# Attention scores by seven block products, partial sums copied out of the PSUM banks, and a fixed order of all engines in attention

## The chip, the cores and the metric

The kernel runs on one core of a Trainium2 chip. The core has a matrix engine (TensorE, PE in the profile, with its weight loads as PEld), VectorE (DVE), ScalarE (ACT), GpSimd (POOL) and SyncE (SP, which issues transfers). Matrix products are written to PSUM, 8 banks of 512 fp32 values a partition; all other data of a stage lies in SBUF. The metric is the time of one execution on the device in microseconds.

## What is computed

A macaron block on x of shape (2, 2048, 256) in fp32: half a feed-forward, attention, half a feed-forward, each on the layer norm of x, each added to x.

```python
x = x + 0.5 * ffn(layernorm(x), w_gate, w_up, w_down)
x = x + attn(layernorm(x), Wq, bq, Wk, bk, Wv, bv, Wo, bo)
x = x + 0.5 * ffn(layernorm(x), w_gate, w_up, w_down)

def ffn(x, w_gate, w_up, w_down):          # every operand rounded to fp4 in blocks of 16, 704 hidden
    h = silu(fp4_linear(x, w_gate)) * fp4_linear(x, w_up)
    return fp4_linear(h, w_down)

def attn(x, ...):                          # one head; complex q, k, v of 256 each, so 512 real columns
    scores = (qr @ kr.T + qi @ ki.T) / sqrt(256)
    w = softmax(scores)
    return stack([w @ vr, w @ vi]) @ Wo.T + bo
```

## The kernel before

The 4096 tokens are 32 tiles of 128, 16 for each batch element ("batch" below). The kernel runs the first feed-forward (FFN0), the attention and the second feed-forward (FFN1), which overlap at their seams. Query and key weights are folded into one 256 x 256 matrix `wa`, value and output weights into `wvo`, so attention works on the normalised x itself: `xT` (x transposed, the keys) and `xn` (x as it is, the values).

**Attention's steps.** Queries go in 8 groups of 512 (`Group`, four to a batch), keys in `NP = 8` pairs of tiles. A *step* `n = 8 gi + s` is group `gi` against key pair `s`. In step n PE computes

- `scores` (L889): for each of the pair's two key tiles a 128 x 512 block of scores, two matmuls of 512 columns each, into a PSUM bank of `p_acc`; ACT copies the block to SBUF (L896, the *piece* `st`), and DVE takes the running maximum `most` from PSUM (L901);
- `values` (L969) of step n - 10, seven matmuls of 256 columns: the 2 x 2 block product of weights and values is made by seven block products instead of eight (the groups but the last), whose left sides are the `xn` blocks with their sums s1 to s4 (`plain`), and whose right sides are quarters of the piece and sums `tw` of them, made by DVE in `combined` (L933, L936, L937).

In between, the group's maximum is transposed (`peak`, L908), reduced, spread over the partitions (`highest`, L915) and copied by ACT from PSUM to SBUF (`top`, L917). `weights` subtracts it from a piece (DVE, L921) and takes the exponential (ACT, L922), one piece a step, one group behind the scores. When the eight values steps of a group are through, `collect` (L988 to L995) puts the seven products together and `close` (L1002 to L1008) multiplies by `wvo`, divides by the sum of weights and adds to x, four tiles at once.

**PSUM.** `p_big` has two tiles of two banks (the seven products `m`, or a feed-forward's gate and up), `p_t` two banks for all transposes, queries and closings, `p_acc` two banks (scores, last group's values, down projections).

**Other work beside the steps.** Batch 1 is normalised, transposed (`turned`, L826) and laid out (`plain`) during the groups of batch 0, and the first inputs of FFN1 are rounded during the last groups.

**What sets the order.** In FFN0 and FFN1 strings (`FFN0_ORDER`, `FFN1_ORDER`) say which piece of work issues its next instruction, and `fence` holds each engine to that order. In attention there is no such string: a scheduler orders the instructions by their dependencies and by marks, with which `tc.issue_after` (L1019, L1091) ties a step's side work to the step's last maximum or last matmul:

```python
seen, scored = scores(todo[gi], s) if gi < groups else (None, None)
with behind(seen):
    if 0 < gi < groups:
        shifted(todo[gi - 1], s)
```

## Time and profile before

| | |
|---|---|
| three runs | 1030.5, 1031.86, 1032.02 us, median 1031.86 |
| the profiled execution | 1032.48 us, span 1029.9 us, mean granted clock 0.998 |
| PE busy | 1002.9 us, 97% of the span |
| DVE, ACT, POOL busy | 785.6, 418.3, 165.6 us |
| 320 to 770 us (attention alone) | PE 449.2, DVE 317.0, ACT 200.7, POOL 5.8 of 450 us |
| matmuls of the scores (L889) | 512 records, 231.8 us |
| matmuls of the values, seven products (L969) | 784 records, 224.5 us |
| DMA in 320 to 770 us | 1 GB/s |

An fp32 matmul leaves two records on PE, and two weight loads. "Busy" is the share of time in which an engine executes; for PE the ends of records are modelled. In the groups, a line names the source line, the engine, the operation, the tiles (out<-in) and the shapes, then busy time and the mean duration of one in ns, then the engine's idle time just before it and what ended that. The chain of waits follows the work that ended last back to the start; the timeline gives start and length of each instruction, with the idle time before it and its releaser in brackets.

### The profile page before, as it was taken

To read this page: it belongs to the slowest core of one execution; us is meant where nothing else is said; L and a number is where in the kernel's file an instruction comes from. 1 tells how busy PE (TensorE), PEld (TensorE's weight loads), DVE (VectorE), ACT (ScalarE), POOL (GpSimd) and SP (SyncE) were. 2 spreads that over 40 slices of the span, in tenths; PEclk is the share of its full clock that TensorE was granted. 3 is DMA by queue.
4 is the path that set the end of the run, shared out by engine and by line. 5 is a ranking of instruction groups with operands and counts; after the bars stand their busy time and mean duration, and the time that the engine had idled before them with its cause. 6 is when DMAs were issued, how large, how long until landed. Compare 5 with 4: busy or idle time off the path is not lost.

```text
span 1029.9 us, 10476 instructions
## 1 busy us (share of the span) xinstructions
PE 1002.9 (97%) x3813; PEld 690.7 (67%) x3813; DVE 785.6 (76%) x1329; ACT 418.3 (41%) x651; POOL 165.6 (16%) x94
## 2 busy tenths in 40 slices
PE   5999999999999999999999999999999999999997
PEld 3667667767665667667676766666655666776776
DVE  7999999969744977476677867677757389988895
ACT  5755533343326543246444533343333244333121
POOL 4464133131220000000000000000002102133321
PEclk9999999999999999999999999999999999999999
DMA  9001246433420000000000000000000033664552
GB/s 321 9 1 48 65 100 108 94 84 63 100 59 1 1 0 1 1 1 0 1 1 1 0 1 1 1 0 1 1 0 1 11 74 92 123 138 109 125 122 57
DMA packets 59285, 49.30 MB, mean 48 GB/s; under 512 B 46050, under 2 KB 51171, under 8 KB 58851
## 3 DMA queue, kind: packets, MB, share of 16 engines
q1 hardware_dynamic: 58272, 48.11, 20.1%
q10 hardware_dynamic: 962, 0.53, 0.2%
q8 instruction: 30, 0.49, 0.2%
q14 instruction: 21, 0.16, 0.0%
HBM read 8.46 MB, written 4.19 MB: 12 GB/s over the span
## 4 chain that ended last, share of the span: by engine, by line
PE 83%; DVE 12%; ACT 2%; issue 1%; DMA 1%; ACTq 0%; DVEq 0%
PE gu L525 22%; PE ps L889 21%; PE m L969 16%; PE po L581 13%; PE poa L1002 3%; PE z L947 3%; PE pu L871 3%; DVE h L242 2%; DVE qh_s L223 1%; PE th L566 1%; DVE bn L321 1%; PE txa L826 1%; DVE h L234 1%; DVE h L543 1%; DMA x<-in_x_dram 1%
## 5 line engine op out<-in xcount | busy, mean ns | idle before, releaser
L525 PE MATMUL gu<-wgu,xqT 128*128 128x352 f32 x992 | 305.7, 460 | 2.7 <-issue 0.7
L525 PEld LDWEIGHTS gu<-wgu,xqT 128*128 128x128 f32 x992 | 185.5, 190 | 101.3 <-issue 5.7
L889 PE MATMUL ps<-uT,xT 128*128 128x512 f32 x512 | 231.8, 593 | 0.2
L581 PE MATMUL po<-wd,hqT 128*128 128x256 f32 x768 | 175.4, 382 | 0.0
L581 PEld LDWEIGHTS po<-wd,hqT 128*128 128x128 f32 x768 | 145.3, 192 | 26.0 <-issue 2.4
L889 PEld LDWEIGHTS ps<-uT,xT 128*128 128x128 f32 x512 | 95.4, 190 | 94.3 <-issue 80.0
L901 DVE TENSOR_TENSOR most<-ps,most 128x512 f32<-128x512 f32 x112 | 77.3, 690 | 104.4 <-ACT st L896 104.0
L896 ACT COPY st<-ps 128x512 f32<-128x512 f32 x128 | 74.6, 583 | 153.3 <-PE ps L889 153.2
L969 PE MATMUL m<-tw,xn 128*128 128x256 f32 x448 | 124.5, 379 | 0.0
L251 POOL TENSOR_TENSOR hqT<-hqT,qh_t 128x1408 f32<-128x1408 f32 x24 | 76.0, 3166 | 191.9 <-DMA qh_t<-h 145.2
L969 PE MATMUL m<-st,xn 128*128 128x256 f32 x336 | 100.0, 379 | 0.0
L969 PEld LDWEIGHTS m<-tw,xn 128*128 128x128 f32 x448 | 85.1, 190 | 12.5 <-DVE tw L933 0.6
L922 ACT ACTIVATE st<-st 128x1024 f32<-128x1024 f32 x64 | 67.2, 1056 | 64.4 <-DVE st L921 64.1
L539 ACT ACTIVATE h<-gu 128x704 f32<-128x704 f32 x62 | 46.6, 756 | 102.5 <-PE gu L525 99.1
L543 DVE TENSOR_TENSOR h<-h,gu 128x704 f32<-128x704 f32 x62 | 54.3, 878 | 40.9 <-PE gu L525 31.2
L969 PEld LDWEIGHTS m<-st,xn 128*128 128x128 f32 x336 | 63.3, 190 | 26.1 <-issue 19.1
L921 DVE TENSOR_TENSOR st<-st,top 128x1024 f32<-128x1024 f32 x64 | 77.0, 1216 | 2.4 <-ACT top L917 2.4
L303 POOL TENSOR_TENSOR xl<-xl,qx_s 128x1024 f32<-128x1024 f32 x4 | 7.8, 1944 | 381.7 <-DVE xl L301 381.7
L239 ACT ACTIVATE qh_m<-h 128x1408 f32<-128x1408 f32 x24 | 33.0, 1376 | 57.5 <-DVE h L234 37.3
L234 DVE SCALAR_TENSOR_TENSOR h<-h,qh_r 128x1408 f32<-128x1408 f32 x24 | 49.0, 2043 | 0.3
L583 DVE SCALAR_TENSOR_TENSOR x<-po,x 128x256 f32<-128x256 f32 x64 | 26.1, 413 | 30.2 <-PE po L581 30.2
L242 DVE SCALAR_TENSOR_TENSOR h<-qh_m,h 128x1408 f32<-128x1408 f32 x24 | 42.6, 1776 | 1.8 <-ACT qh_m L239 1.8
(181 smaller groups left out, 1115.1 us busy)
## 6 DMA issues: line engine op xcount, KB each, us to landing
hqT<-eight SPq DMA_DIRECT2D x24, 704.0 KB
xqT<-eight SPq DMA_DIRECT2D x9, 512.0 KB
out_dram<-x SPq DMA_DIRECT2D x15, 256.0 KB
x<-in_x_dram SPq DMA_DIRECT2D x3, 1024.0 KB
eight<-whole SPq DMA_DIRECT2D x24, 44.0 KB
wd<-wd SPq DMA_DIRECT2D x2, 384.0 KB
n_down<-in_w_down_dram SPq DMA_DIRECT2D x1, 704.0 KB
n_up<-in_w_up_dram SPq DMA_DIRECT2D x1, 640.0 KB
```

The source lines that it names most:

```text
L234: nc.vector.scalar_tensor_tensor(yb, yb, BELOW, rec.unsqueeze(2).to_broadcast([P, nb, BLK]), ALU.mult, ALU.mult)
L242: nc.vector.scalar_tensor_tensor(y, m, LEAST, y, ALU.max, ALU.add)
L251: nc.gpsimd.tensor_tensor(state["dst"], state["dst"], crossed, ALU.mult)
L525: nc.tensor.matmul(out=ps[:, b2, 0:HALF], lhsT=xqT[:, i % XT, kc, :], rhs=wgu[:, kc, ts(which * 2 + b2, HALF)], start=(kc == 0), stop=(kc ...
L543: nc.vector.tensor_tensor(h, h, up, ALU.mult)
L581: nc.tensor.matmul(out=po, lhsT=hqT[:, r, :], rhs=right, start=(k == 0), stop=(k == NR - 1))
L889: scored = nc.tensor.matmul(out=ps, lhsT=gr.of.xT[s][:, c, v, :], rhs=gr.uT[:, c, :], start=(c == 0), stop=(c == KD - 1),)
L896: nc.scalar.copy(piece[:, v, :], ps)
L901: seen = nc.vector.tensor_tensor(gr.most, ps, gr.most, ALU.max)
L921: nc.vector.tensor_tensor(piece, piece, gr.top.unsqueeze(1).to_broadcast([P, 2, Q]), ALU.subtract)
L922: nc.scalar.activation(piece, piece, AF.Exp, scale=SCALE)
L969: i = nc.tensor.matmul(out=gr.m[k], lhsT=left, rhs=right, start=first, stop=last)
```

## The change

**Scores.** For steps n = 10 to 63 (`PLAIN = 10` and on) a new function `step(n)` takes the place of `scores`, `shifted`, `combined`, `values`, `queries`, `close` and `peak` in the loop. The pair's two key tiles and the two halves of the 256 features form a 2 x 2 block matrix, the group's queries (two halves of 256 queries) another; their product is made by seven block products of 256 columns instead of four matmuls of 512. The partial sums share registers: `px` and `pz` are the halves of the step's bank `ps`, `py` is the second half of the bank of the step before. `px` is read three times while it accumulates: after products 1 (ACT, L1212), 2 (ACT, L1230) and 3 (DVE, L1248); `pz` twice (ACT L1213, DVE L1237). The fourth product into `px` is issued in the next step (`deferred`, L1164) and copied there (L1215).

**Sums of keys and queries.** The left sides need four sums of key blocks a pair (`halves`, tiles `xS`), the right sides four sums a group (`halved`, in `uT`), all on POOL. The four sums of the value step move from DVE to POOL (`combined`), one of them in place in the piece.

**Maxima.** `most` is now taken from the piece's two halves in SBUF (L1251 for the upper, `seen_lower` in the next step for the lower). `top` stays in PSUM: the ACT copy goes, and DVE's subtraction (`lowered`, L1048) reads it there. While a top is held, transposes, queries and closings have one bank of `p_t` instead of two (`bank`).

**Order.** The whole region n = 10 to 63 is fenced: every engine executes its instructions in the order in which `step` writes them. Side work (batch 1's statistics, `turned`, `halves` and `plain`, FFN1's first inputs) is cut into turns, and `spare` issues turns at three places of a step, up to a budget for each engine (0.7 and 1.25 us of DVE; 2.0 us for each of ACT, DVE, POOL and PE at the end). Closings are made one tile at a time in steps s = 3 and 4, queries at s = 2 (or 4 and 5).

**Smaller parts.** The ring of pieces has 11 places instead of 12; `xn` has 7 blocks instead of 8, one of them restored by POOL for the last group; the reciprocal root of the variance is a power on POOL for batch 1 and FFN1's first groups instead of ACT's square root and DVE's reciprocal.

The diff, cut to its core (lines that only pass `bank` for the pool, and `queries`, `close`, `plain` cut into turns, are left out):

```diff
+    def bank(shape, name):
+        passing["turn"] ^= 1
+        tag = "t1" if passing["top"] or passing["turn"] else "t0"
+        return p_t.tile(shape, FP, tag=tag, name=name)
...
+            if self.power:
+                nc.gpsimd.tensor_tensor(rstd, var, minus_half[:, 0:n], ALU.pow)
+                yield "W"
+            else:
+                nc.scalar.activation(sd, var, AF.Sqrt)
+                yield
+                nc.vector.reciprocal(rstd, sd)
+                yield
...
+            y = xl.rearrange("p u d -> p (u d)")
+            nb = XT * D // BLK
+            yb = y.rearrange("p (b k) -> p b k", k=BLK)
+            yield "W", 0
+            yield "D", 1.2
+            scale = xp.tile([P, nb], FP, tag="qx_s", name="qx_s", bufs=2)
+            nc.vector.tensor_reduce(scale, yb, AX.X, ALU.max, apply_absolute_value=True)
+            yield "D", 0.7
+            rec = xp.tile([P, nb], FP, tag="qx_r", name="qx_r", bufs=2)
+            nc.vector.tensor_scalar(scale, scale, 1.0 / 6.0, TINY, ALU.mult, ALU.max)
+            nc.vector.reciprocal(rec, scale)
+            yield "D", 1.2
+            by_block = rec.unsqueeze(2).to_broadcast([P, nb, BLK])
+            nc.vector.scalar_tensor_tensor(yb, yb, BELOW, by_block, ALU.mult, ALU.mult)
+            yield "A", 1.0
+            m = xp.tile([P, XT * D], FP, tag="qx_m", name="qx_m", bufs=1)
+            nc.scalar.activation(m, y, AF.Abs, scale=STEPS)
+            yield "W", 0
+            yield "D", 1.2
+            nc.vector.scalar_tensor_tensor(y, m, LEAST, y, ALU.max, ALU.add)
+            yield "D", 1.2
+            nc.vector.scalar_tensor_tensor(y, m, LEAST, y, ALU.max, ALU.subtract, reverse1=True)
+            yield "W", 0
+            yield "G", 1.9
+            nc.gpsimd.tensor_tensor(yb, yb, scale.unsqueeze(2).to_broadcast([P, nb, BLK]), ALU.mult)
+            yield "W", 0
...
+        def halves(self, p, pool):
+            yield "W", 0
+            x, t = self.xT[p], pool.tile([P, 4, P], FP, tag=f"xS{p}", name=f"xS{self.b}_{p}")
+            self.xS[p] = t
+            a11, a12, a21, a22 = x[:, 0, 0, :], x[:, 1, 0, :], x[:, 0, 1, :], x[:, 1, 1, :]
+            add = nc.gpsimd.tensor_tensor
+            yield "G", 0.9
+            add(t[:, 0, :], a21, a22, ALU.add)
+            add(t[:, 1, :], t[:, 0, :], a11, ALU.subtract)
+            yield "G", 0.9
+            add(t[:, 2, :], a11, a21, ALU.subtract)
+            add(t[:, 3, :], a12, t[:, 1, :], ALU.subtract)
+        def restored(self, p):
+            yield "G", 0.6
+            a11, s3 = self.xn[p][:, 0, :], self.xn[p][:, 1, :]
+            nc.gpsimd.tensor_tensor(s3, a11, s3, ALU.subtract)
+            nc.gpsimd.memset(s3[:, P - 1:P], 1.0)
...
-    RING = NP // 2 + LAG
+    RING = NP + LAG + 1
+    EARLY = 6
+    PLAIN = NP + LAG
...
+        def halved(gr):
+            b11, b12, b21, b22, t1, t2, t4 = (gr.uT[:, k, :] for k in range(7))
+            add = nc.gpsimd.tensor_tensor
+            add(t1, b12, b11, ALU.subtract)
+            yield
+            add(t2, b22, t1, ALU.subtract)
+            yield
+            add(t4, b21, t2, ALU.subtract)
+            yield
+            add(b12, b22, b12, ALU.subtract)
+            yield
...
+            passing["top"] = True
+            gr.top = p_t.tile([P, QG, P], FP, tag="t0", name=f"top{gr.i}")
             for u in range(QG):
-                nc.tensor.transpose(pt[:, u, :], gr.mx[:, u:u + 1].to_broadcast([P, P]), ident)
-            gr.top = late["pool"].tile([P, Q], FP, tag="top", name=f"top{gr.i}")
-            nc.scalar.copy(gr.top, pt.rearrange("p u s -> p (u s)"))
+                nc.tensor.transpose(gr.top[:, u, :], gr.mx[:, u:u + 1].to_broadcast([P, P]), ident)
+        def lowered(gr, s):
+            piece = gr.pieces[s]
+            top = gr.top.rearrange("p u s -> p (u s)").unsqueeze(1).to_broadcast([P, 2, Q])
+            nc.vector.tensor_tensor(piece, piece, top, ALU.subtract)
+        def raised(gr, s):
+            piece = gr.pieces[s]
+            nc.scalar.activation(piece, piece, AF.Exp, scale=SCALE)
         def weights(gr, s):
-            piece = gr.pieces[s]
-            nc.vector.tensor_tensor(piece, piece, gr.top.unsqueeze(1).to_broadcast([P, 2, Q]), ALU.subtract)
-            nc.scalar.activation(piece, piece, AF.Exp, scale=SCALE)
+            lowered(gr, s)
+            raised(gr, s)
...
-        def combined(gr, s):
-            piece = gr.pieces[s]
-            b = piece.rearrange("p v (h q) -> p (v h) q", h=2)
-            t = late["pool"].tile([P, 4, HQ], FP, tag="tw", name=f"tw{gr.i}_{s}", bufs=2)
-            nc.vector.tensor_tensor(
-                t[:, 0:2, :], b[:, 0:4:3, :], b[:, 1:2, :].to_broadcast([P, 2, HQ]), ALU.add
-            )
-            nc.vector.tensor_tensor(t[:, 3, :], t[:, 1, :], b[:, 0, :], ALU.add)
-            nc.vector.tensor_tensor(t[:, 2, :], t[:, 3, :], b[:, 2, :], ALU.add)
-            gr.t[s] = t
...
+        def combined(gr, s, engine):
+            b = gr.pieces[s].rearrange("p v (h q) -> p (v h) q", h=2)
+            gr.t[s] = t = late["pool"].tile([P, 3, HQ], FP, tag="tw", name=f"tw{gr.i}_{s}", bufs=2)
+            add = engine.tensor_tensor
+            add(t[:, 0, :], b[:, 0, :], b[:, 1, :], ALU.add)
+            add(b[:, 1, :], b[:, 3, :], b[:, 1, :], ALU.add)
+            add(t[:, 1, :], b[:, 1, :], b[:, 0, :], ALU.add)
+            add(t[:, 2, :], t[:, 1, :], b[:, 2, :], ALU.add)
...
+        def deferred():
+            gr, s, ps, piece, _ = pend.pop("fourth")
+            nc.tensor.matmul(
+                out=ps[:, 0:HQ], lhsT=gr.of.xT[s][:, 1, 1, :], rhs=gr.uT[:, 6, :], start=False, stop=True,
+                skip_group_check=True,
+            )
+        def seen_lower(gr, s, piece):
+            if s == 0:
+                nc.vector.tensor_tensor(most_of(gr), piece[:, 1, :], piece[:, 0, :], ALU.max)
+            else:
+                nc.vector.tensor_tensor(gr.most, piece[:, 1, :], gr.most, ALU.max)
+        def step(n):
+            gi, s = divmod(n, NP)
+            gr, old = todo[gi], todo[gi - 1]
+            gv, sv = divmod(n - NP - LAG, NP)
+            valued = sevenfold(todo[gv], sv)
+            x, sums, u = gr.of.xT[s], gr.of.xS[s], gr.uT
+            a11, a12, a21, a22 = x[:, 0, 0, :], x[:, 1, 0, :], x[:, 0, 1, :], x[:, 1, 1, :]
+            piece = room(gr, s)
+            b = piece.rearrange("p v (h q) -> p (v h) q", h=2)
+            if "bank" not in pend:
+                pend["bank"] = p_acc.tile([P, Q], FP, tag="acc", name="ps")
+            ps = p_acc.tile([P, Q], FP, tag="acc", name=f"ps{gi}_{s}")
+            before = pend["bank"]
+            px, pz, py = ps[:, 0:HQ], ps[:, HQ:Q], before[:, HQ:Q]
+            asks = gi + 1 < groups and (gi + 1) % (tiles // QG) != 0
+            if s == 2 and gi + 1 < groups:
+                todo[gi + 1] = Group(gi + 1)
+            ahead = todo.get(gi + 1)
+            def times(out, left, right, start=False, stop=False):
+                nc.tensor.matmul(out=out, lhsT=left, rhs=right, start=start, stop=stop, skip_group_check=True)
+            def v(k):
+                for _ in range(k):
+                    next(valued, None)
+            late_one = s in (0, 2)
+            if s == 3 and asks or s == 6 and ahead and not asks:
+                all_of(halved(ahead))
+            times(px, a11, u[:, 0, :], True)
+            times(pz, sums[:, 0, :], u[:, 4, :])
+            fourth = pend.get("fourth")
+            if fourth:
+                deferred()
+            nc.scalar.copy(b[:, 0, :], px)
+            nc.scalar.copy(b[:, 3, :], pz)
+            if fourth:
+                nc.scalar.copy(fourth[4], before[:, 0:HQ])
+            if "exp" in pend:
+                raised(*pend.pop("exp"))
+            cs, cn = divmod(n - NP - LAG + 1, NP)
+            combined(todo[cs], cn, nc.gpsimd)
+            early = not late_one and n > NP + LAG
+            if early:
+                lowered(old, s)
+            spare(n, "D", 0.7)
+            if s == 2 and asks:
+                queries(ahead, 0)
+            elif s != 2:
+                v(1)
+            times(px, sums[:, 1, :], u[:, 5, :])
+            times(pz, sums[:, 3, :], u[:, 3, :])
+            nc.scalar.copy(b[:, 1, :], px)
+            if fourth:
+                seen_lower(fourth[0], fourth[1], fourth[3])
+            v(1)
+            if s == 0:
+                pt = peak(old)
+            v(1)
+            nc.vector.tensor_tensor(b[:, 1, :], pz, b[:, 1, :], ALU.add)
+            if s == 0:
+                peaked(old, pt)
+            times(px, sums[:, 2, :], u[:, 1, :])
+            times(py, a12, u[:, 2, :], True, True)
+            if early:
+                raised(old, s)
+            if s == 0:
+                highest(old)
+            else:
+                spare(n, "D", 1.25)
+            nc.vector.tensor_tensor(b[:, 3, :], px, b[:, 3, :], ALU.add)
+            nc.vector.tensor_tensor(b[:, 0, :], py, b[:, 0, :], ALU.add)
+            if s > 0:
+                nc.vector.tensor_tensor(gr.most, piece[:, 0, :], gr.most, ALU.max)
+            if s == 2 and asks:
+                queries(ahead, 1)
+            if late_one and n > NP + LAG:
+                lowered(old, s)
+                pend["exp"] = old, s
+            if s in (3, 4) and "closing" in pend:
+                close(pend["closing"], 2 * (s - 3))
+            v(7)
+            if s in (4, 5) and ahead and not asks:
+                queries(ahead, s - 4)
+            if s in (3, 4) and "closing" in pend:
+                close(pend["closing"], 2 * (s - 3) + 1)
+                if s == 4:
+                    pend.pop("closing")
+            if sv == NP - 1:
+                pend["closing"] = todo.pop(gv)
+                collect(pend["closing"])
+            pend["bank"] = ps
+            pend["fourth"] = gr, s, ps, piece, b[:, 2, :]
+            spare(n, "ADGP", 2.0)
...
+            if PLAIN <= n < groups * NP:
+                if n == PLAIN:
+                    begun = len(nc.cur_bb.bb.instructions)
+                step(n)
+                if n == groups * NP - 1:
+                    fourth = pend["fourth"]
+                    deferred()
+                    nc.scalar.copy(fourth[4], fourth[2][:, 0:HQ])
+                    seen_lower(fourth[0], fourth[1], fourth[3])
+                    peaked(fourth[0], peak(fourth[0]))
+                    fence(begun)
+                yield None, None
+                continue
...
+    def spare(n, kinds, most):
+        left = {kind: most for kind in kinds}
+        for task in list(asides):
+            if task[0] > n:
+                continue
+            if task[2][0] == "W":
+                task[2] = next(task[1], None)
+            while task[2] is not None and task[2][0] in left and task[2][1] <= left[task[2][0]]:
+                left[task[2][0]] -= task[2][1]
+                task[2] = next(task[1], None)
+            if task[2] is None:
+                asides.remove(task)
+            elif task[2][0] != "W":
+                left.pop(task[2][0], None)
...
+    def turned(b, p):
+        turns = batches[b].turned(p, kt)
+        for kind in "AAWPP":
+            yield kind, 0.5
+            if kind != "W":
+                next(turns)
+        yield from batches[b].halves(p, late["pool"])
...
+    LED = 4
+    for p in range(LED, NP):
+        aside(EARLY + p, batches[0].plain(p, late["pool"]))
+    for p in (6, 7, 0, 1):
+        aside(PLAIN, batches[0].halves(p, late["pool"]))
+    for part in range(tiles // GT):
+        aside(PLAIN, counted(batches[1].measure(part)))
+    for p in range(NP):
+        aside(per - NP + 1 + p, turned(1, p))
+    for p in range(NP):
+        aside(per + LAG + 1 + p, batches[1].plain(p, late["pool"]))
+    aside(per + NP + LAG + 2, first_inputs())
+    for p in range(NP):
+        aside((groups - 1) * NP + LAG + 1 + p, batches[NB - 1].restored(p))
```

## The prediction

> **What bounds the kernel now.** I read the table of engines first, then the chain that ended last, the stretches, the groups, and one step of attention instruction by instruction. TensorE (PE) is busy 97% of the span, so what counts is the time in which it works or waits:
>
> ```profile
> PE 1002.9 (97%) x3813; PEld 690.7 (67%) x3813; DVE 785.6 (76%) x1329; ACT 418.3 (41%) x651; POOL 165.6 (16%) x94
> PE gu L525 22%; PE ps L889 21%; PE m L969 16%; PE po L581 13%; PE poa L1002 3%; PE z L947 3%; PE pu L871 3%; DVE h L242 2%; DVE qh_s L223 1%; PE th L566 1%; DVE bn L321 1%; PE txa L826 1%; DVE h L234 1%; DVE h L543 1%; DMA x<-in_x_dram 1%
> ```
>
> The stretches show that inside attention PE has no gap at all and GpSimd (POOL) next to no work (columns: stretch, length, busy time of PE, weight loads, DVE, ACT, POOL, granted clock):
>
> ```profile
> 350.00:400.00 50.00, 50.00 (x181) 33.33 (x180) 38.60 (x93) 19.33 (x27) 0.00 (x0) 1.00 0.00 1
> 650.00:700.00 50.00, 50.00 (x190) 34.35 (x189) 34.22 (x57) 20.33 (x31) 0.63 (x1) 1.00 0.00 1
> ```
>
> The chain there is a plain alternation of a step's scores (8 records) and values (14 records), start and length in us:
>
> ```profile
> 603.10 3.43 PE ps L889 x8
> 606.53 3.02 PE m L969 x14
> 609.55 3.43 PE ps L889 x8
> ```
>
> So a step costs PE 3.43 + 3.02 = 6.45 us, and nothing else costs anything. One fp32 matmul is two records: 3.43/4 = 0.858 us for 512 columns, 3.02/7 = 0.432 for 256. The durations of what the change touches (mean ns behind the bar):
>
> ```profile
> L896 ACT COPY st<-ps 128x512 f32<-128x512 f32 x128 | 74.6, 583 | 153.3 <-PE ps L889 153.2
> L921 DVE TENSOR_TENSOR st<-st,top 128x1024 f32<-128x1024 f32 x64 | 77.0, 1216 | 2.4 <-ACT top L917 2.4
> L922 ACT ACTIVATE st<-st 128x1024 f32<-128x1024 f32 x64 | 67.2, 1056 | 64.4 <-DVE st L921 64.1
> L988 ACT COPY u<-m x7: 354/372/373, 385.9 to 738.8; 128x256 f32<-128x256 f32 x7
> L991 DVE TENSOR_TENSOR u<-m,u x7: 415/417/423, 388.5 to 740.7; 128x256 f32<-128x256 f32 x7
> ```
>
> And the handovers, from the step at 662, with start and length:
>
> ```profile
> 662.38 3.60 PE L889 MATMUL ps<-uT,xT 128*128 128x512 f32 x8
> 664.35 0.58 ACT L896 COPY st<-ps 128x512 f32<-128x512 f32 x1 [1.26 <-PE ps L889]
> 664.97 0.69 DVE L901 TENSOR_TENSOR most<-ps,most 128x512 f32<-128x512 f32 x1 [1.45 <-ACT st L896]
> 702.35 0.89 PE L1002 MATMUL poa<-wvo,zT 128*128 128x257 f32 x3 [0.60 <-DVE x L1008]
> ```
>
> The first two matmuls end at 662.38 + 1.72 = 664.10; ACT starts 0.25 later (0.20 in the median, where no event is waited for as well); DVE starts 0.04 after ACT's end (664.93). The L1008 before 702.35 ended at 702.20 (start 701.72, 0.48 long): DVE to PE 0.15 with two waits; elsewhere 0.055 with one.
>
> **The change, part by part.**
>
> *Seven products.* For n = 10 to 63, 54 steps, four matmuls of 512 become seven of 256: 7 x 0.432 = 3.02 instead of 3.43. Gain 0.41 x 54 = 22.3 us if PE stays without a gap.
>
> *The partial sums.* They are read while the accumulation goes on, and every such read stands on PE's path, since the next product into that bank waits for it. The order on PE becomes: px, pz (1, 2); the fourth product of the step before, in another bank (3); a value (4); px, pz (5, 6); two values (7, 8); px (9); py in the other bank (10); four values. The waits attached to the changed instructions: (5) waits for ACT, that is for both copies L1212 and L1213; (9) waits for DVE's add L1237, which reads pz next to px and itself waits for the copy L1230. Two gaps follow:
> - 2 to 5: PE has (3) and (4), 0.863 us. Needed: 0.20 + 0.055 (L1212 waits for two more semaphores) to the first copy's start, 0.272 to the start of the next (0.372 less 0.10 of overlap, as ACT's back-to-back copies start), 0.372, and 0.055 back to PE: 0.95, with another event on the second wait 0.99. Stall 0.13. At s=2 the first query matmuls stand here, 1.73 us, and hide it. 47 steps: 6.1 us.
> - 6 to 9: again 0.863. Needed: 0.20 + 0.372 + 0.03 + 0.418 + 0.055 = 1.08. Stall 0.21, and 0.27 with one more event; I take 0.24. At s=0 four transposes hide it. 48 steps: 11.5 us.
> - 10 to the next 1: L1248 and L1249, 0.20 + 0.33 + 0.42 + 0.06 = 1.0, under 1.73 us of values. Nothing.
>
> Bounds: both hidden, 0; or both 0.15 longer for further events and queued work, 17.6 + 0.15 x 95 = 32 us.
>
> *ACT's queue.* A step has four copies of 256 and an exp: 4 x 0.37 + 1.06 = 2.5 of 6 us. But what is put between the exp and L1212 delays L1212 and, through (5), PE. For n = 26 to 32 the asides of batch 1 put the copy of xT (0.58) and two norms (0.50 apart) there: the transposes end with the step, so the copy starts 0.20 into the next one and L1212 comes at 0.20 + 0.58 + 1.04 = 1.82 instead of 1.16. 7 x 0.66 = 4.6 us. At n = 48 and 54 the Abs of FFN1's input (1.06) waits for DVE's product before it (1.21) and stands ahead of L1212: some 1.65 each, 3.3. None of the three existed as a stall before, where the scheduler placed them; bounds 0 and twice.
>
> *DVE's queue.* Out go a step's sums for the values (three instructions, 0.68 + 0.42 + 0.47 by the groups tw); in come three adds of 0.42; the two maxima of 0.69 stay, now from SBUF alone. So DVE holds 1.22 + 1.26 + 1.38 = 3.9 of 6.4 us, and is no bound. The statistics of batch 1 at n = 44 to 45 and the row of one closing tile stand ahead of L1237 once: 1.3, between 0 and 2.6.
>
> *POOL.* The four sums of 256 move here, with the halves of keys and queries. Trace rows of POOL give 1.06 us for 512 and 2.59 for 1408, undisturbed, so 0.19 us + 1.7 ns an element: 0.63 for 256, as an estimate (the ends: 0.5, half of 1.06, and 1.06 itself). 4 x 0.63 + gaps = 2.8 of 6.4 us, with the halves of keys (4 x 0.41) or queries (4 x 0.63) 4.6 to 5.5, with FFN1's product (1.95) 4.8: it fits, and the results are wanted a step later; at 1.06 it would not in those steps, which the rival below prices. The power that takes the place of a root and a reciprocal for batch 1 has no row; it works on 8 elements a partition, so between 0.2 (POOL's copies of 4) and 1.2 (its smallest sum), and is wanted some steps later: 0. The table loads of 1.28 that the root cost ACT go with it, gain 0 to 2.6, taken as 0, for ACT's idle time before its copies was 153 us. No DMA is issued in these steps and SP's queue is passed by nothing. What speaks against POOL is the company:
>
> ```profile
> 699.37 1.95 POOL L303 TENSOR_TENSOR xl<-xl,qx_s 128x1024 f32<-128x1024 f32 x1 [49.87 <-DVE xl L301]
> 699.84 1.76 DVE L937 TENSOR_TENSOR tw<-tw,st 128x256 f32<-128x256 f32 x1
> ```
>
> L937, 0.42 otherwise, took 1.76 and ended 0.28 after POOL, while the L901 at 546.86, one input of which is in PSUM, kept its 0.69 inside POOL's L303 of 545.39 to 547.33. Of the new DVE work only the two maxima have both inputs in SBUF. The first stands ahead of L1237 with 0.3 to 0.5 us to spare, one add of POOL is 0.63: a quarter of the steps may lose 0.2, 2.7 us at most; I take 0 and keep 2.7 in the range. Weighed against the Trainium skill, "SBUF — State Buffer", section "Who interferes with whom": there a VectorE instruction with two SBUF inputs contends with a GpSimd instruction that reads SBUF, and the loser is blocked for a whole instruction. This is what the row shows. By that rule read strictly, each maximum that meets an add would lose up to 0.63, and the sum would be 0.3 x 54 = 16 us worse; by the row and the slack it is the 0 to 2.7 above.
>
> *Small ones.* Start of the new order at n = 10, whose sums DVE still made: +1. The end of n = 63, where the last product, its copy, a maximum and the transposes follow one another: 0.43 + 0.2 + 0.37 + 0.69 + 0.1 = 1.8, less what PE does meanwhile: +1.45. PE's own few stalls of before (two of 0.17, one of 0.77) go: -1.1. The single bank for transposes while the maximum stays in PSUM, the pieces' ring of 11, and FFN1's inputs: each has a step of time to spare; 0, bounds -2 and +3.
>
> Sum: -22.3 + 6.1 + 11.5 + 4.6 + 3.3 + 1.3 + 1.0 + 1.45 - 1.1 = +5.9. The profiled execution took 1032.48 (span 1029.9, 2.6 around it), 0.6 above the median of 1031.86; so about 1038.4 by its clock, 1037.8 in the median. I say 1038.
>
> **The rivals.**
> - *The copies are hidden* (faster). If the handovers between 2 and 5 and between 6 and 9 are 0.13 and 0.24 shorter than added up, both gaps vanish: -22.3 + 10.6 = -11.7; without the waits in ACT's queue too, -19.6. Time 1012 to 1020. For it: the gaps are small beside the 1.0 us that I added up, and the weight loads go ahead of a waiting matmul, as the timeline of before shows. Against: each part of the sums is a measured row. It decides at 11.7/54 = 0.22 us of both gaps together in a step: below that the change gains.
> - *POOL and DVE hold each other up.* If the first maximum mostly meets an add, or POOL takes 1.06 rather than 0.63 and the values wait for its sums, 0.3 to 0.5 us a step: +16 to +27 more, 1054 to 1065. For it: L937's 1.76. Against: DVE's adds on the path read PSUM.
> - *Gain and waits cancel.* Gaps 0.06 shorter each: 5.9 - 0.06 x 95 = 0.2, time 1032.
>
> **How the numbers follow.** My case, gaps as worked out within 0.05, 1034 to 1050: 0.50. POOL against DVE: 0.14. Hidden: 0.28. About equal: 0.08 (within 0.2%, 2 us, about what a measurement of this kernel can tell from no change). Slower 0.64, faster 0.28, same 0.08. The range leaves out the far part of the two outer rivals, one in ten each: 1018 to 1057. My case alone has 1034 to 1050.
>
> **What would show it.** The product steps take 6.04 + 0.37 = 6.4 us, with two waits of PE in each, one released by ACT's L1213 (0.1) and one by DVE's L1237 (0.2 to 0.3); PE's share falls by 2 to 3 points; gaps above 0.6 us stand at n = 26 to 32 behind the copy of xT. I am wrong if PE is without gaps in these steps, if PE waits for POOL in the values, or if a maximum L1171/L1173 takes over 1 us in most steps.

## The result and the profile after

The changed kernel takes 1059.72 us in the median, the kernel before beside it 1031.94: a ratio of 1.0271, 95% interval 1.0253 to 1.0289. So it is slower, as forecast, but by 27.8 us instead of 6, and 2.7 us beyond the end of the range. The profiled execution took 1060.47 us with a span of 1057.9, 28.0 more than before.

Busy engines and the chain of the changed kernel, from the page:

```profile
PE 1007.5 (95%) x4137; PEld 743.4 (70%) x4137; DVE 812.2 (77%) x1328; ACT 409.4 (39%) x742; POOL 398.5 (38%) x446
PE 68%; DVE 19%; ACT 7%; issue 3%; POOL 2%; DMA 1%; DVEq 0%; ACTq 0%; POOLq 0%
PE gu L590 22%; PE po L646 12%; PE ps L1197 11%; PE m L1092 10%; PE poa L1141 3%; PE ps L1015 2%; PE pu L969 2%; PE z L1111 2%; DVE st L1237 2%; DVE h L252 1%; ACT st L1230 1%; ACT st L1052 1%; DVE bn L331 1%; PE ps L1164 1%; DVE st L1048 1%
```

The same line of the kernel before:

```profile
PE 83%; DVE 12%; ACT 2%; issue 1%; DMA 1%; ACTq 0%; DVEq 0%
```

PE's share of the chain fell from 83% to 68%; in its place stand DVE and ACT, with L1237 and L1230 by name. The two stretches of attention, columns as before:

```profile
350.00:400.00 50.00, 47.38 (x212) 37.96 (x211) 40.42 (x89) 17.71 (x40) 31.59 (x49) 1.00 0.00 1
650.00:700.00 50.00, 46.52 (x207) 37.52 (x208) 35.24 (x57) 18.46 (x41) 26.62 (x31) 1.00 0.00 1
```

Where PE had no gap, it now has 2.6 and 3.5 us in 50. One quiet step shows how. It is n = 22, in the timeline of the changed kernel (start, length):

```profile
426.96 0.59 PE L1197 MATMUL ps<-uT,xT 128*128 128x256 f32 x2
...
428.10 0.37 ACT L1212 COPY st<-ps 128x256 f32<-128x256 f32 x1 [3.46 <-POOL tw L1067]
428.25 0.59 PE L1092 MATMUL m<-st,xn 128*128 128x256 f32 x2
428.37 0.38 ACT L1213 COPY st<-ps 128x256 f32<-128x256 f32 x1
...
428.80 1.13 PE L1197 MATMUL ps<-uT,xS 128*128 128x256 f32 x4
...
429.06 1.10 DVE L1173 TENSOR_TENSOR most<-st,most 128x512 f32<-128x512 f32 x1 [1.34 <-ACT st L1215]
...
430.20 0.59 PE L1092 MATMUL m<-st,xn 128*128 128x256 f32 x2
...
430.44 0.42 DVE L1237 TENSOR_TENSOR st<-ps,st 128x256 f32<-128x256 f32 x1 [0.29 <-ACT st L1230]
430.92 0.30 PEld L1197 LDWEIGHTS ps<-uT,xS 128*128 128x128 f32 x2 [0.53 <-DVE st L1237]
430.92 0.70 PE L1197 MATMUL ps<-uT,xS 128*128 128x256 f32 x2
431.24 0.41 PEld L1197 LDWEIGHTS ps<-uT,xT 128*128 128x128 f32 x2
431.46 0.59 PE L1197 MATMUL ps<-uT,xT 128*128 128x256 f32 x2
```

Product 5 could start at 428.25 + 0.43 = 428.68 and starts at 428.80, after L1213; product 9 could start at 430.63 and starts at 430.92, after L1237. These are the two gaps of the prediction, 0.11 and 0.29 long. There is a third item that it had not: after a wait, the two records of the next matmul are 0.32 apart instead of 0.216 (430.92 and 431.24; the pair is 0.70 long instead of 0.59). The weight loads show why. Elsewhere a load starts one record, 0.216, ahead of the pass that it serves (the load at 431.24 for the pass at 431.46). The first load of product 9 waits for L1237 as its matmul does and starts together with it, at 430.92; the load of the second pass comes 0.11 after that, and its pass again 0.21 later. So a wait that holds back the load too costs 0.10 us more than it is long; this is called a restart below. The step takes 433.62 - 426.96 = 6.66 us: 6.04 of products, 0.11 + 0.29 of waits, 0.2 of restarts.

### The profile page after: what moved, and what is told of

Same layout as the page of the kernel before. It is cut to its first block, busy times and chain, and to the rows that moved or that the text cites. A ratio compares the mean times of both kernels' runs of the same rounds, so it can differ in the third digit from the quotient of the medians.

```text
span 1057.9 us, 11721 instructions
## 1 busy us (share of the span) xinstructions
PE 1007.5 (95%) x4137; PEld 743.4 (70%) x4137; DVE 812.2 (77%) x1328; ACT 409.4 (39%) x742; POOL 398.5 (38%) x446
## 4 chain that ended last, share of the span: by engine, by line
PE 68%; DVE 19%; ACT 7%; issue 3%; POOL 2%; DMA 1%; DVEq 0%; ACTq 0%; POOLq 0%
PE gu L590 22%; PE po L646 12%; PE ps L1197 11%; PE m L1092 10%; PE poa L1141 3%; PE ps L1015 2%; PE pu L969 2%; PE z L1111 2%; DVE st L1237 2%; DVE h L252 1%; ACT st L1230 1%; ACT st L1052 1%; DVE bn L331 1%; PE ps L1164 1%; DVE st L1048 1%
## 5 line engine op out<-in xcount | busy, mean ns | idle before, releaser
L1197 PE MATMUL ps<-uT,xS 128*128 128x256 f32 x432 | 130.6, 405 | 17.0 <-ACT st L1213 8.0
L1092 PE MATMUL m<-st,xn 128*128 128x256 f32 x448 | 131.8, 379 | 0.0
L1197 PEld LDWEIGHTS ps<-uT,xS 128*128 128x128 f32 x432 | 74.4, 190 | 60.3 <-DVE st L1237 27.8
L1092 PE MATMUL m<-tw,xn 128*128 128x256 f32 x336 | 100.5, 381 | 1.6 <-DVE tw L1069 1.6
L1067 POOL TENSOR_TENSOR tw<-st 128x256 f32<-128x256 f32 x54 | 40.1, 743 | 163.3 <-PE m L1092 93.3
L1092 PEld LDWEIGHTS m<-st,xn 128*128 128x128 f32 x448 | 84.1, 190 | 10.9
L1173 DVE TENSOR_TENSOR most<-st,most 128x512 f32<-128x512 f32 x48 | 43.1, 897 | 48.4 <-ACT st L1215 46.3
L1048 DVE TENSOR_TENSOR st<-st,top 128x1024 f32<-128x1024 f32 x64 | 76.5, 1211 | 0.1
L1212 ACT COPY st<-ps 128x256 f32<-128x256 f32 x54 | 20.0, 370 | 135.9 <-PE ps L1197 92.4
L1092 PEld LDWEIGHTS m<-tw,xn 128*128 128x128 f32 x336 | 64.0, 191 | 10.8 <-DVE tw L1069 2.0
L1197 PE MATMUL ps<-uT,xT 128*128 128x256 f32 x216 | 64.4, 380 | 0.4 <-DVE most L1026 0.4
L261 POOL TENSOR_TENSOR xqT<-xqT,qx_t 128x1024 f32<-128x1024 f32 x9 | 20.4, 2263 | 104.0 <-DMA qx_t<-qx_q 61.1
```

The costliest lines, as they stand in the source:

```text
L261: nc.gpsimd.tensor_tensor(state["dst"], state["dst"], crossed, ALU.mult)
L1048: nc.vector.tensor_tensor(piece, piece, top, ALU.subtract)
L1067: add(t[:, 0, :], b[:, 0, :], b[:, 1, :], ALU.add)
L1092: i = nc.tensor.matmul(out=gr.m[k], lhsT=left, rhs=right, start=first, stop=last)
L1173: nc.vector.tensor_tensor(gr.most, piece[:, 1, :], gr.most, ALU.max)
L1197: nc.tensor.matmul(out=out, lhsT=left, rhs=right, start=start, stop=stop, skip_group_check=True)
```

## Where the 28 us lie

Excess here is the distance between the starts of two PE records less the undisturbed one (0.108, 0.216 or 0.429 us by width), summed from the trace. Attention from the first value record to the last group's first: 406.4 us before (333.8 to 740.2), 433.6 after (337.1 to 770.8).

| term | predicted, us | measured, us |
|---|---|---|
| products | -22.3 | -22.3 |
| before product 5, quiet steps | 6.1 | 5.5 (50 x 0.11) |
| before product 9, quiet steps | 11.5 | 13.1 (0.22 to 0.29) |
| restart after each wait | none | 9.8 (94 x 0.104) |
| ACT's queue: copy of xT, n = 26 to 33 | 4.6 | 4.1 |
| ACT's queue: Abs, n = 48 and 54 | 3.3 | 4.0, and 1.7 of half clock |
| DVE's queue ahead of L1237 | 1.3 | 3.5 (n = 12, 13, 15, 26, 45) |
| one bank for closings, queries, transposes | 0 | 5.5 |
| the start, to n = 10 | 1.0 | 5.3 |
| the end of n = 63 | 1.45 | 1.44 |
| stalls of before that go | -1.1 | -2.1 |
| after attention | 0 | -2.5 |

The rest, 1.0 us, are 0.4 more ahead of product 5 at n = 58 and waits of some 0.1 each ahead of the maxima's transposes. Where the 2.5 us after attention come from stays open.

Two of these as the timeline of the changed kernel shows them. At n = 48 the Abs of FFN1's input (L570) waits for DVE, L1212 (at 638.23) and L1213 stand behind it, and product 5 behind these:

```profile
637.26 1.06 ACT L570 ACTIVATE qx_m<-xl 128x1024 f32<-128x1024 f32 x1 [4.46 <-DVE xl L567]
...
638.48 0.38 ACT L1213 COPY st<-ps 128x256 f32<-128x256 f32 x1
...
638.91 1.28 PEld L1197 LDWEIGHTS ps<-uT,xS 128*128 128x128 f32 x4 [2.37 <-ACT st L1213]
```

And in n = 28, where batch 1's queries, a closing and the transposes share one bank, each waits until the one before has been read out of it (by L976, then by L1147):

```profile
483.24 1.14 PE L1141 MATMUL poa<-wvo,zT 128*128 128x257 f32 x4 [0.68 <-ACT uT L976]
...
485.25 0.63 PE L895 MATMUL txa<-ident,nat 128*128 128x128 f32 x4 [0.87 <-DVE x L1147]
```

## The experiments

**Products or order.** Only the seven products are undone; order, side work, POOL's sums and the maximum in PSUM stay:

```diff
-            times(px, a11, u[:, 0, :], True)
-            times(pz, sums[:, 0, :], u[:, 4, :])
...
+            block(ps, 0)                       # two matmuls of 512
+            nc.scalar.copy(piece[:, 0, :], ps)
...
+            block(second, 1)
+            nc.scalar.copy(piece[:, 1, :], second)
```

> The fixed order, the side work, POOL's sums and the maximum in PSUM stay; only the seven products of the scores are undone: four matmuls of 512 with two banks, a copy of 512 for each. Theory: PE's work grows by 22.3 us, the waits at products 5 and 9 with their restarts (29.5 + 10.8 us) go but for a few: 1041 to 1046, with 6 to 10 us of waits left in the special steps (closings and transposes in one bank, the start at n = 10). Rival (the order and the side work cost the time): the waits stay, 1060 or more. If the order costs nothing at all: 1032.

Measured: 1039.08 us, ratio to before 1.0072 (1.0057 to 1.0087), a little below the 1041 to 1046 forecast. The waits at px are gone; what is left are the start (2.9 us in one wait) and the single bank. So of the 28 us some 7 stay without the seven products, and 20.6 go with them, although they save PE 22.3 us of work: they cost PE some 43 us of waiting, of which the trace has 41.2 ahead of products 5 and 9 and in their restarts. Not all of this belongs to the partial sums alone: with the products go their copies and DVE's three adds, and with these the places where side work stands ahead of them. What moving the side work gives with the products kept, the run e5_side_work below shows.

**The wait before product 9.** One value more between products 6 and 9:

```diff
                 pt = peak(old)
-            v(1)
+            v(2)
```

> Three values instead of two stand between products 6 and 9 (and three instead of four after 10), so PE has 1.295 us there instead of 0.863; the handover through L1230 and L1237 needs about 1.1. Theory (two handovers a step leave PE waiting, and each wait costs about 0.09 more when PE starts again, because the weights of its second pass are loaded only then): the wait before 9 goes in 48 steps, 48 x (0.26 + 0.09) = 17 us; after 10 the remaining 1.295 us still cover the 1.0 us of L1248 and L1249. About 1043 us. Rival (the fixed order and the side work cost the time, the waits only move): 1056 to 1060. Rival (POOL and DVE hold each other up): the wait is longer than one matmul in many steps, so 1047 to 1055.

Measured: 1047.16 us, ratio 1.0151 (1.0134 to 1.0169), 4 us above the forecast. The waits before product 9 fell from 16.6 to 5.1 us, the restarts by 4.1, and 2.4 came back ahead of the closings' second tiles, which now have three values instead of four behind the first. The time is also the lower end of the rival of POOL and DVE, but that rival's waits in many steps are not there: the 5.1 us stand in 7 steps (n = 12 to 15, 26, 42 and 45). The same place of the step in this run:

```profile
429.42 0.37 ACT L1230 COPY st<-ps 128x256 f32<-128x256 f32 x1 [0.94 <-PE ps L1197]
429.89 0.42 DVE L1237 TENSOR_TENSOR st<-ps,st 128x256 f32<-128x256 f32 x1 [0.29 <-ACT st L1230]
430.37 0.33 PEld L1197 LDWEIGHTS ps<-uT,xS 128*128 128x128 f32 x2
430.51 0.59 PE L1197 MATMUL ps<-uT,xS 128*128 128x256 f32 x2
```

L1237 ends at 430.31, the weights of product 9 load from 430.37, it starts at 430.51 in its turn, 0.14 behind its load, and its pair is 0.59 long again.

**The wait before product 5.** One copy for px and pz:

```diff
-            nc.scalar.copy(b[:, 0, :], px)
-            nc.scalar.copy(b[:, 3, :], pz)
+            nc.scalar.copy(b[:, 0:4:3, :], ps.rearrange("p (h q) -> p h q", h=2))
```

> px and pz leave their bank in one ACT copy of 512 (0.585 us) instead of two of 256 (0.37, the second 0.27 after the first). Theory: the first wait, before product 5, falls from 0.11 to about 0.03 and its restart cost of 0.09 stays where any wait is left: 47 x 0.08 = 4 us, 1056; if it goes entirely, 47 x 0.20 = 9 us, 1050. Either rival: no change, 1058 to 1061.

Measured: 1058.00 us, ratio 1.0255 (1.024 to 1.0271). The time alone does not tell this from no change: its interval overlaps that of the changed kernel, and it is what the rivals said. The trace does: the wait fell from 0.11 to 0.05 (0.03 was worked out), and the 0.10 of the restart stayed, so of 0.21 us a step 0.16 are left.

**POOL against DVE.** The four sums go back to DVE in one run; two of them are made twice on POOL in another:

```diff
-            combined(todo[cs], cn, nc.gpsimd)
+            combined(todo[cs], cn, nc.vector)
```

> The four sums for the values go back to DVE; POOL is empty in most steps. Theory (handovers): the maxima L1173 and L1251 fall to 0.69 us each, but the wait before 9 stays at 0.22 or more, for it is made of ACT's copy and DVE's add; DVE has 1.6 us more a step, 5.5 of 6.6, and where its sums stand ahead of L1237 the wait grows: 1060 to 1085. Rival (POOL and DVE hold each other up): the wait before 9 falls below 0.1, 1045 to 1050.

Measured: 1137.27 us, ratio 1.1037 (1.1004 to 1.1069), 52 us beyond the end of the forecast. The maxima are free of POOL, but DVE's sums wait for exponentials and stand ahead of L1237: the waits before product 9 rose to 76.6 us, up to 3.8 in a step, and about 13 us more are stretches at half clock behind such waits (mean granted clock 0.983). Apart from s = 0, where the transposes cover it, no step had less than 0.22, so the handover is there without POOL too.

```diff
             add(t[:, 0, :], b[:, 0, :], b[:, 1, :], ALU.add)
+            add(t[:, 0, :], b[:, 0, :], b[:, 1, :], ALU.add)
...
             add(t[:, 2, :], t[:, 1, :], b[:, 2, :], ALU.add)
+            add(t[:, 2, :], t[:, 1, :], b[:, 2, :], ALU.add)
```

> The changed kernel with two of POOL's four sums made twice in every step (the same values again): 1.5 us more POOL work, 4.4 of 6.6. Theory (handovers through PSUM): DVE's adds on PE's path have one input in PSUM and keep 0.42 us, so 1059 to 1062. Rival (POOL and DVE hold each other up): the maxima rise above 1.0 us and the waits before 9 with them, 0.1 to 0.2 us a step: 1065 to 1071.

Measured: 1066.60 us, ratio 1.0351 (1.0326 to 1.0375), inside the rival's numbers, but without its sign: the maxima did not rise above 1.0 us. The maximum `seen_lower` (min, median, max in ns; its line moves by two with the added sums) with the sums on DVE, in the changed kernel, and with POOL's extra sums:

```profile
L1173 DVE TENSOR_TENSOR most<-st,most x48: 674/685/942, 350.5 to 837.3; 128x512 f32<-128x512 f32 x48
```
```profile
L1173 DVE TENSOR_TENSOR most<-st,most x48: 677/948/1235, 346.7 to 763.0; 128x512 f32<-128x512 f32 x48
```
```profile
L1175 DVE TENSOR_TENSOR most<-st,most x48: 678/922/2090, 348.8 to 768.1; 128x512 f32<-128x512 f32 x48
```

POOL does hold the maxima up, 0.26 us in the median, and more sums on POOL don't add to that. But the quiet steps keep their 0.29: in n = 22 above, L1173 took 1.10 and ended at 430.16, and L1237 waited for the copy until 430.44. The medians are 6.9 us apart, the two profiled executions 5.4. Of these, 3.6 are waits before product 9, and 2.9 of those at n = 12 alone: there DVE waits 2.24 us for POOL's power (L341), which stands behind the doubled sums, and only then lays out batch 0 and comes to L1237. Another 1.1 are a longer wait for DVE's own sums at n = 10, two of which the edit doubles as well. So this rival is real where DVE's queue waits for POOL ahead of L1237, and not in the ordinary step.

**The side work** (e5_side_work). Its places in the step change; products, copies and values stay:

```diff
+            yield "W", 0                       # the Abs one spare place later
             yield "A", 1.0
...
+            spare(n, "P", 1.0)                 # transposes right behind product 10
...
+            po = projected(pend["closing"], 2 * (s - 3)) if s in (3, 4) and "closing" in pend else None
...
-            spare(n, "ADGP", 2.0)
+            spare(n, "ADG", {"A": 2.0, "D": 0.9 if s in (3, 4) else 2.0, "G": 2.0})
```

> The steps' products, copies and values stay as changed (two waits a step); only the side work moves: the Abs of FFN1's input a spare place later, the transposes of x and their copy right behind product 10, the first tile of each closing pair among the values before product 9, two values ahead of batch 1's queries, and 0.9 instead of 2.0 us of DVE's spare work at the end of steps with a closing. Theory: what stood in ACT's queue ahead of L1212 goes (7 x 0.5 + 2 x 2.0 + 1.9 of half clock), the waits in the one bank (4.8), DVE's bursts (2.4): 16 us, 1043. Rival (the side work was hidden and all comes from the two waits): 1057 to 1060.

Measured: 1040.39 us, ratio 1.009 (1.0073 to 1.0107): 19.3 us, against 16 forecast. The waits before product 5 fell from 14.3 to 7.1 us. Those before product 9 fell too, from 16.6 to 13.7 with 1.25 of restarts: in 12 steps a closing's first tile now stands between products 6 and 9 and hides the wait.

**Side work, values 1, 3, 3 and one copy together** (e6_no_waits), then with the start and the end (e7_all):

> The side work as in the run before, the values 1, 3, 3 and one copy for px and pz. Theory: 1043 less 16.5 (the wait before 9 with its restarts) less 3: 1023, so below the kernel before; PE's excess in attention below 10 us. Rival (the handovers come back elsewhere, after product 10 or in the values): 1033 or more.

Measured: 1028.42 us, ratio 0.9971 (0.9962 to 0.998), faster than both, but not the 1023 forecast. The quiet steps take 6.20 us: 6.04, a wait of 0.05 and its restart of 0.10. PE's excess in attention is 20.4 us, not below 10: 8.7 are still ahead of product 5 (3.6 of waits, 5.1 of restarts) and 6.9 ahead of product 9 in crowded steps.

```diff
+            with ExitStack() as order:         # the marks of the kernel before
+                for mark in marks:
+                    if mark is not None:
+                        order.enter_context(tc.issue_after(mark))
...
+            if n == groups * NP - 1:
+                v(1)
+                pend["fourth"] = gr, s, ps, piece, b[:, 2, :]
+                deferred()
```

> As the run before, and batch 0's layout is tied to its step again by marks, as in the kernel before, and the last fourth product is issued ahead of the last values. Theory: 2.5 at the start and 1.4 at the end less: 1019.

Measured: 1029.38 us, ratio 0.9981 (0.9971 to 0.999): a miss. The first value came 1.2 us earlier, and the steps from there on took 405.4 instead of 401.9 us. The loss stands in n = 10, which took 15.9 us instead of 11.4: its values wait 2.5 us for DVE's sums instead of 1.8, product 9 waits 1.0, and the granted clock is 0.66 from 338 to 348 us. The end of n = 63 did gain: the last maximum's transposes wait 0.58 us instead of 1.44.

**pz and py change banks** (e9_other_bank), so that a product of the other bank and values stand between a read and the next product into the bank that is read:

```diff
-            px, pz, py = ps[:, 0:HQ], ps[:, HQ:Q], before[:, HQ:Q]
+            px, py, pz = ps[:, 0:HQ], ps[:, HQ:Q], before[:, HQ:Q]
...
-            times(pz, sums[:, 0, :], u[:, 4, :])
             fourth = pend.get("fourth")
             if fourth:
                 deferred()
+            times(pz, sums[:, 0, :], u[:, 4, :], True)
...
             times(px, sums[:, 2, :], u[:, 1, :])
-            times(py, a12, u[:, 2, :], True, True)
+            v(2)
+            times(py, a12, u[:, 2, :], False, True)
```

> pz and py change places: pz goes into the second half of the bank of the step before, py into the step's own. The order becomes px, the fourth product of the step before, pz, two values, px, pz, one value, px, two values, py, two values. Between a product and the next one into its bank PE then has 1.3, 0.86, 0.86 and 1.3 us of other work, and each handover behind it is one copy (0.20 + 0.37 + 0.06 = 0.63), one add (0.67) or two copies (0.95). Side work as in e5_side_work. Theory: all regular waits with their restarts go, 1028.4 of e6_no_waits less 7 and some of DVE's bursts: 1018 to 1021. Rival (a wait of this kind always comes back next to another one): 1028 or more.

Measured: 1038.57 us, ratio 1.0077 (1.0056 to 1.0098): a miss in the sum and a hit in the mechanism. Every quiet step now takes 6.04 us, without a wait. But the special steps lost more than that: waits before closings (8 x 0.5), before transposes (4 x 1.37), before the maxima's transposes (5.1) and at px behind DVE's bursts (4.3). The timeline of this run shows one reason:

```profile
430.96 0.59 PE L1204 MATMUL ps<-uT,xT 128*128 128x256 f32 x2
...
431.59 0.42 DVE L1252 TENSOR_TENSOR st<-ps,st 128x256 f32<-128x256 f32 x1 [1.63 <-PE ps L1204]
```

L1252 reads px, finished at 430.1, but it was written behind py, and py lies in the same bank: it waited for py's end. These lines are from a quiet step; in a step with a closing, the closing's work on DVE stands behind it.

The same banks and products without the other places of the side work:

> The changed kernel with that order of banks and products alone; side work, its places in the step and the two closings as changed, but DVE's spare work of 1.25 us stands behind L1249 instead of ahead of L1248. Theory: the regular waits were 40 x 0.20 + 47 x 0.36 = 25 us with restarts, so 1035; the side work's 15 us stay. Rival (the side work is worth more once the waits are gone, or less): outside 1030 to 1040.

Measured: 1047.97 us, ratio 1.0171 (1.0152 to 1.019); 11.8 us less than the changed kernel, not 25, and outside 1030 to 1040, as the rival said. The side work did cost more here: the two Abs hold PE up for 3.4 us each instead of 2.1, and each closing's second tile waits 0.7 or more.

And with e9_other_bank's work on DVE in another order:

> As e9_other_bank, with four things moved on DVE and PE: L1248 and the closing's two instructions are written ahead of py (so they wait for px alone), DVE's spare work at a step's end is 0.7 instead of 2.0 us, and the maximum's transposes stand after the third px. Theory: the waits that e9_other_bank has left are DVE's queue and not PSUM: before the closings' second tile 10 x 0.5, before transposes 4 x 1.37, before the maxima 5.1, before px behind DVE's bursts 4.3; some 16 to 18 of 20 us go: 1021 to 1024. Rival (with the shorter steps DVE itself has become the bound): the waits come back at the next step's px, 1030 or more.

Measured: 1031.31 us, ratio 0.9999 (0.9989 to 1.0008), a third miss: 7.3 us gained of the 15 to 18. The listed waits went, and others took their place ahead of py of the same step (10.1 us in 12 steps), with 2.6 us at n = 58 behind ACT's L1219; the 2.6 at n = 10 had been there before. The 10.1 us end with L1247, DVE's read of px in the bank that py goes into. So DVE has not finished with a bank when a product wants it, much as that rival said, though it named px of the next step; which of DVE's instructions would have to move stays open.

**DVE's side work thinned out**, on the best version so far (e6_no_waits):

```diff
-            spare(n, "ADG", {"A": 2.0, "D": 0.9 if s in (3, 4) else 2.0, "G": 2.0})
+            spare(n, "ADG", {"A": 2.0, "D": 0.9, "G": 2.0})
...
-        aside(PLAIN, counted(batches[1].measure(part)))
+        aside(PLAIN + 6, counted(batches[1].measure(part)))
```

> As e6_no_waits, with batch 1's statistics from n = 16 on instead of n = 10, and DVE's spare work at every step's end 0.9 instead of 2.0 us. Theory (what e6_no_waits has left in its special steps is DVE's queue ahead of L1237): the waits of 0.33, 0.36, 1.25 and 0.94 us at n = 12 to 15 and 0.67 and 1.02 at n = 45 to 50, with 0.1 for each restart, fall to a third: 3 to 4 us, 1024 to 1026. Rival (the statistics hit L1237 wherever they stand): 1028 or more.

Measured: 1024.59 us, ratio 0.993 (0.9916 to 0.9943): as forecast, and the fastest, 35 us below the changed kernel with the same seven products. The waits before product 9 fell from 5.8 to 1.6 us. Attention and its seams (320 to 770 us) in the changed kernel and here:

```profile
320.00:770.00 450.00, 424.50 (x1865) 335.29 (x1866) 310.73 (x577) 170.24 (x361) 229.69 (x341) 1.00 0.00 1
```
```profile
320.00:770.00 450.00, 443.59 (x1978) 358.86 (x1979) 342.69 (x635) 189.66 (x332) 237.01 (x345) 1.00 0.00 1
```

PE goes from 25.5 idle microseconds to 6.4 in the same stretch, at the same clock in its mean; restarts are not among them, since a record is longer by them.

## Why the prediction was right in kind and wrong in size

- **Bound and gain.** Right: PE's work fell by 22.3 us, and the waits on partial sums are what ate it.
- **The two handovers.** Right to a tenth of a microsecond: 0.13 predicted and 0.11 measured, 0.24 and 0.22 to 0.29. The two waits of PE are the first two of their kind in the view of waits (us in total, times, longest), the special steps included; this is idle time of the weight loads, which run ahead of the matmuls, so that the 0.53 of n = 22 stands for a wait of 0.29:

```profile
PEld ps L1197 <- DVE st L1237: 27.8, 47, 1.7
...
PEld ps L1197 <- ACT st L1213: 25.7, 49, 2.4
```

- **The step that failed first** is the one that takes a wait's cost for its length ("0.055 back to PE"): each of the 94 waits cost 0.104 more in the restart, 9.8 us, a term that the sum did not have. It stood in the trace of before. There the first load behind the wait starts with its pass, at 334.38; the second pass follows at 334.91, with the load for the pass behind it, and that one at 335.34, so 0.53 later and then the usual 0.43:

```profile
334.38 1.55 PE L889 MATMUL ps<-uT,xT 128*128 128x512 f32 x3
334.38 0.30 PEld L889 LDWEIGHTS ps<-uT,xT 128*128 128x128 f32 x2 [0.43 <-DVE most L901]
334.91 0.19 PEld L889 LDWEIGHTS ps<-uT,xT 128*128 128x128 f32 x1 [0.24 <-issue]
```

  I had read where waits end and not what follows. The run with one copy and the one with values 1, 3, 3 show it from both sides: a wait of 0.05 keeps the whole restart, and a handover that ends 0.2 us ahead of the matmul's turn has none.
- **"The single bank ... each has a step of time to spare; 0, bounds -2 and +3"** was wrong: 5.5 us. The bank has a step's time on average, but closings, queries and transposes come in the same steps, one right behind the other.
- **"Start of the new order: +1"** was 5.3. I looked at n = 10 and priced it at 1; it cost 2.9, 1.8 of them in values that wait for DVE's sum. The two steps before it, from which the change took the marks, cost another 2.9, and 0.5 of before go: there, norms of batch 0's layout stand ahead of ACT's copies and its sums ahead of DVE's maxima, for which PE is idle 1.18 and 1.24 us (both behind L1026). The wait of n = 10 (1.59 idle, 1.75 by the distance of the starts):

```profile
339.31 0.70 PE L1092 MATMUL m<-tw,xn 128*128 128x256 f32 x2 [1.59 <-DVE tw L1069]
```

  With the marks back the first value came 1.2 us earlier, and n = 10 lost more than that, most of it at half clock; what would mend the start stays open.
- **ACT's queue**: 4.6 and 3.3 against 4.1 and 4.0; the half clock after the long wait, 1.7 us, was not foreseen. **DVE's queue**: 1.3 against 3.5, beyond its end of 2.6.
- **POOL.** Its add of 256 took 0.73 us where 0.63 was estimated; the results came in time, and this cost nothing.
- **The rivals.** That the copies are hidden fell; one of its reasons, that weight loads go ahead of a waiting matmul, does not hold at the wait shown above. That POOL and DVE hold each other up holds for the maxima (the lower one took over 1 us in 20 of 48 steps, not in most), but was not the cause of the quiet steps' waits; it counts where DVE is crowded.
- **The range** reached to 1057 through the rival of POOL and DVE; the three terms put at nothing, 0 and 1 (restart, bank, start) measured 20.6 us together, and little in the range stood for them.

## What to carry to other kernels

Reading a partial sum while its bank is still being written puts a chain of engines on TensorE's path: copy, add, and two crossings were 0.9 to 1.1 us here, so it takes two to three matmuls of other work behind each such read, and a handover that ends too late for the next weights to load ahead, some 0.1 us before the matmul's turn, costs a restart on top, however short the wait is. Before counting saved matmuls, count the independent ones that are left to fill these places: here eight for three places that want nine, until products were sent to the other bank. And what is written into a fixed order between two quiet steps (a copy that waits for PE, a burst of statistics) delays whatever stands behind it on that engine, so side work is priced by who queues behind it, not by its engine's idle time.

## What the runs showed of the hardware

After a wait, an fp32 matmul's second pass comes late by what the lead of its first weight load is short of some 0.1 us, and not by the wait's length: 0.104 where load and matmul start together (waits of 0.05 as of 2 us), 0.08 with a lead of 0.03 (702.35 in the kernel before), 0.05 with 0.05 (596.32 in e12_dve_later), 0.03 with 0.08 (461.33 in e10_other_bank_alone), and nothing with 0.14 (430.51 in e1_values_1_3_3). And an idle PE can lose its clock: after the 2.1 us wait at n = 48, records were twice as far apart for 3.4 us, with the granted clock (the column behind the busy times) at 0.57, and at 1.00 again after that:

```profile
639.00:643.00 4.00, 4.00 (x13) 3.28 (x14) 1.54 (x3) 0.50 (x2) 0.36 (x1) 0.57 0.00 0
643.00:646.00 3.00, 3.00 (x18) 2.64 (x17) 2.81 (x5) 0.00 (x0) 0.00 (x0) 1.00 0.00 0
```

The equally long wait at n = 54 of the same execution was not followed by this (1.00 from 685 to 692 us); with values 1, 3, 3 it was the other way round. The Trainium skill, "TensorE: Matmul & The Clock Gate", section "Part 1: The HAM clock gate", has the half clock follow an idle window of about 3.4 us that runs freely. A free window would fit the 3.4 us and the chance by which of two waits it strikes; that the wait was only 2.1 us long does not fit, and there the measurement decides. Why the one wait has it and the other not, the runs don't show. DVE's maximum with both inputs in SBUF took 0.95 us in the median beside POOL's sums and 0.69 without; adds with one input in PSUM kept 0.42 throughout. This agrees with what the Trainium skill says of the two engines' shared port ("SBUF — State Buffer", section "Who interferes with whom").
